# A routed expert layer: rows gathered by a list of nodes instead of scattered to their places

## The chip, the cores and the metric

The kernel runs on one core of a Trainium2 chip. A core has a matrix engine (TensorE, PE), a vector engine (VectorE, DVE), a scalar engine (ScalarE, ACT), a general engine (GpSimd, POOL) and a sequencer that mostly issues transfers (SyncE, SP). Each engine takes its own instructions in order, and engines wait for each other by semaphores. Sixteen DMA engines move data between the large memory (HBM) and the on-chip memory (SBUF). TensorE writes its results to a small accumulation memory (PSUM).

The metric is device microseconds (us) of one execution, as the median over runs. Three runs of the kernel before are given: 5335.9, 5335.99 and 5341.02 us, with a median of 5335.99 us.

## The reference, cut to what matters

The program takes 625 nodes with 512 features and 10,000 edges through eight layers. Each adds its result to the nodes. The change lies in the second of them, an attention block followed by a layer in which each node is sent to one of eight experts:

```python
h = _layernorm(x + o, ln1_g, ln1_b)            # o: output of the attention
t = h.reshape(b * s, d)                        # 625 x 512
probs = jax.nn.softmax(t @ gate_W + gate_b, axis=-1)
idx = jnp.argmax(probs, axis=-1)               # one of 8 experts per node
gw = jnp.max(probs, axis=-1)
hid = jax.nn.gelu(jnp.einsum('nd,edf->enf', t, W1) + b1[:, None, :])
out_all = jnp.einsum('enf,efd->end', hid, W2) + b2[:, None, :]
onehot = jax.nn.one_hot(idx, E, dtype=t.dtype)
out = jnp.einsum('ne,end->nd', onehot, out_all)
out = out * gw[:, None]
```

W1 is 8 x 512 x 2048 and W2 is 8 x 2048 x 512, all in float32.

## The kernel before, in words

The kernel is one program of eight phases, one function each, run one after the other. The nodes stay in SBUF as `C.x`, five tiles of 125 nodes (`NT` = 5, `P` = 125) by 512 features. The second phase is `L0_ffn`.

**Experts with 128 places each.** A node goes only through the expert that its gate chose. Each expert has 128 places (`SLOTS`), so 8 x 128 = 1024 places in all, and a node's place number is `slot` = 128 times its expert plus its rank among that expert's nodes. A node whose rank is 128 or more gets a number of its own beyond 1024 and is left to a second routine, `L0_late`, which runs only if some expert has more than 128 nodes (line 898). `slot` is made on DVE from the one-hot choice `oh` with two small products on PE (lines 784 and 785) that count the nodes before each one; `to` is `slot` as an integer (line 797).

**How the rows reach their experts.** The layer's input rows `t_tok` are in SBUF by node. Lines 798 to 800 scatter them: for each of the five node tiles, one indirect transfer issued by POOL writes 125 rows of 2 KB to `places` in HBM, at the rows that `to` gives. All five write the same HBM tensor. Lines 801 to 803 then load the eight experts' 128 rows from `places` into eight buffers `at_e`, by transfers that SP issues. So that unused places hold numbers, SP fills `places` with zeros early in the phase (lines 724 and 725), beside the zeros for `made`, the HBM tensor that takes the experts' results (lines 726 to 728).

**What follows.** PE turns each expert's rows with four transposes into `xg`, features by places (line 823); DVE and ACT take turns copying the results out of PSUM (lines 179 and 181 in the helper `copy`). Then the experts run. The weights come through a ring of six 1 MB buffers (`ring`, line 682): 64 loads, two for each of 32 steps. The first six are issued at the start of the phase, and each later one is issued when a buffer is released. `first` (line 843) multiplies a step's W1 part, ACT applies the activation (line 848), and `second` (line 857) multiplies the W2 part. The seven first experts' results go to `made`, and `take` (line 872) fetches each node's row from there with five indirect transfers on POOL; the last expert's results are spread by one-hot products (line 881).

**What else the steps below touch.** The attention ends with the layer norm of `t_tok` (`C.layernorm`, lines 153 to 164). The small tensors of the gate live in a pool opened after the attention (`a_r`), whose memory the attention used before, so their first writers wait for the attention. Work is placed on the engines' queues by a scheduler that may move an instruction ahead of or behind others of its engine; the order spoken of in the prediction is the order in the built program. SP's queue holds, in this order, the six ring loads, eight zero fills of `places`, two of `made`, the load of the attention's output weights (`Wo`), the other fills of `made`, the load of the next phase's weights (`w_next`), the eight loads of `at_e`, and the rest of the ring. Two small loads of a much later phase, `wx` and `bsel` (lines 1292 and 1314), are issued by ACT just before the experts start.

Of the kernel before, what the change touches and what calls it, by code (L numbers as in the profile page):

```python
# [15 lines left out]
F32 = mybir.dt.float32  # L16
F16 = mybir.dt.float16
BF16 = mybir.dt.bfloat16
I32 = mybir.dt.int32
U32 = mybir.dt.uint32  # L20
U16 = mybir.dt.uint16
AF = mybir.ActivationFunctionType
ALU = mybir.AluOpType
AX = mybir.AxisListType
# [4 lines left out]
N, D, P, NT = 625, 512, 125, 5  # L29
# [11 lines left out]
SLOTS = 128  # L41
# [614 lines left out]
def L0_ffn(C):  # L656
# [5 lines left out]
    nc, tc, I = C.nc, C.tc, C.ins  # L662
    E8, FF = 8, 2048
# [4 lines left out]
    with ExitStack() as st:  # L668
# [7 lines left out]
        def load(upto):  # L676

            for key in parts[len(loaded):upto]:
# [3 lines left out]
                nc.sync.dma_start(w, src.rearrange("(k p) n -> p k n", p=128))  # L682
                loaded[key] = w


        places = C.dram.tile([E8 * SLOTS + N, D], F32, name="places")
        made = C.dram.tile([E8 * SLOTS + N, D], F32, name="made")
        zero = pool.tile([128, D], F32, name="zero")
        nc.gpsimd.memset(zero, 0.0)
# [2 lines left out]
        t_tok = pool.tile([P, NT, D], F32, name="t_tok")  # L692
        with ExitStack() as st2:
            apool = st2.enter_context(tc.tile_pool(name="aa", bufs=1))
            qT = apool.tile([128, KC, N], F32, name="qT")
            kT = apool.tile([128, KC, N], F32, name="kT")
            v = apool.tile([P, NT, D], F32, name="v")
            with tc.tile_pool(name="a_ps", bufs=2, space=PSUM) as ps:
                xT = apool.tile([128, KC, N], F32, name="xT")
                C.feature_major(ps, xT, xn)  # L700
                bo = C.row_bcast(pool, W("bo"), D, "bias", 2)
                for t in range(NT):
                    nc.gpsimd.tensor_add(xn[:, t], xn[:, t], bo[:P])
                for dst, w, b in ((qT, "Wq", "bq"), (kT, "Wk", "bk")):
                    wt = C.weight(W(w).rearrange("(k p) n -> p k n", p=128), KC)
                    col = C.columns(pool, ps, W(b).rearrange("(c p) -> c p", p=128), KC, "col_" + b)
                    for c in range(KC):
                        for n0, n in HALVES:
                            pq = ps.tile([128, 512], F32, name="pq")
                            C.linear_T(pq[:, :n], xT, n0, n, wt, c)  # L710
                            nc.scalar.activation(dst[:, c, n0:n0 + n], pq[:, :n], AF.Identity,
                                                 bias=col[:, c:c + 1])
                wt = C.weight(W("Wv").rearrange("(k p) n -> p k n", p=128), KC)
                bv = C.row_bcast(pool, W("bv"), D, "bias", 2)
                for t in range(NT):
                    pv = ps.tile([P, D], F32, name="pv")
                    C.linear(pv, xT, t, wt)
                    nc.vector.tensor_add(v[:, t], pv, bv[:P])
            wt = C.weight(W("Wo").rearrange("(k p) n -> p k n", p=128), KC)
            g = C.row_bcast(pool, W("ln1_g"), D, "ln_g")  # L720
            b = C.row_bcast(pool, W("ln1_b"), D, "ln_b")
            st_ = C.small.tile([P, NT, 6], F32, name="ln_st")

            for e in range(E8):
                nc.sync.dma_start(places[e * SLOTS:(e + 1) * SLOTS], zero[:SLOTS])
            for r in range((E8 - 1) * SLOTS, E8 * SLOTS + N, 128):
                n = min(128, E8 * SLOTS + N - r)
                nc.sync.dma_start(made[r:r + n], zero[:n])

            def finish(t, out):  # L730
                for half in range(2):
                    part = xn[:, t, half * 256:(half + 1) * 256]
                    nc.vector.tensor_add(part, part, out[half])
                nc.vector.bn_stats(st_[:, t], xn[:, t])

            C.attention(qT, kT, v, wt, 1.0 / 8.0, False, finish)
            C.layernorm(t_tok, xn, g, b, st_)

        tT = pool.tile([128, KC, N], F32, name="tT")
        sel = pool.tile([P, NT, E8], F32, name="sel")  # L740
# [2 lines left out]
        with ExitStack() as st2:  # L743
            E2 = st2.enter_context
            rpool = E2(tc.tile_pool(name="a_r", bufs=1))
            R = lambda shape, name: rpool.tile(shape, F32, name=name)
            beyond = R([P, NT], "beyond")
            nc.gpsimd.iota(beyond, pattern=[[P, NT]], base=E8 * SLOTS, channel_multiplier=1,
                           allow_small_or_imprecise_dtypes=True)
            place = R([128, E8], "place")  # L750
            nc.gpsimd.iota(place, pattern=[[SLOTS, E8]], base=0, channel_multiplier=1,
                           allow_small_or_imprecise_dtypes=True)
            before = R([P, P], "before")
            nc.vector.tensor_scalar(before, C.iota[:P, :P], place[:P, 0:1], None, op0=ALU.is_gt)
            to = rpool.tile([P, NT], U32, name="to")
            xg = R([128, KC, E8 * SLOTS], "xg")
            srow = R([128, N], "srow")
            slot, rk, gv = R([P, NT], "slot"), R([P, NT], "rk"), R([P, NT], "gv")
            oh, rank, base = (R([P, NT, E8], k) for k in ("oh", "rank", "base"))
            with tc.tile_pool(name="a_ps3", bufs=2, space=PSUM) as ps, tc.tile_pool(name="a_at", bufs=1) as work:  # L760
# [35 lines left out]
                nc.vector.tensor_add(slot, slot, beyond)  # L796
                nc.vector.tensor_copy(to, slot)
                for t in range(NT):
                    nc.gpsimd.indirect_dma_start(out=places[:, :], in_=t_tok[:, t], in_offset=None,
                                                 out_offset=bass.IndirectOffsetOnAxis(ap=to[:, t:t + 1], axis=0))  # L800
                at_e = [work.tile([SLOTS, D], F32, name="at_e", bufs=E8) for e in range(E8)]
                for e in range(E8):
                    nc.sync.dma_start(at_e[e], places[e * SLOTS:(e + 1) * SLOTS])
                top = pool.tile([1, 1], F32, name="top")
                nc.vector.tensor_add(base[0:1, 0], base[0:1, NT - 1], pn[0:1, 1, NT - 1])
                nc.vector.reduce_max(top, base[0:1, 0], axis=AX.X)
# [944 lines left out]


PHASES = [graph_and_L0_gnn, L0_ffn, L1_gnn, L1_ffn, L2_gnn, L2_ffn, L3_gnn, L3_ffn]


# [48 lines left out]
```

## Time and profile before

| what | us |
|---|---|
| median of three runs | 5335.99 |
| the profiled execution | 5344.59 |
| its span, first to last instruction | 5342.8 |
| TensorE busy over the span | 4977.2 (93%) |
| attention's last products, layer norm, gate and ranks: from 427 to 453 | 26 |
| from the first scatter on POOL (453.07) to the first product with W1 (492.50) | 39.4 |
| experts, to the last product with W2 (about 717) | 224 |

The profile is of one execution. A row names line, engine, operation, and result and operands (`places<-t_tok,to`), then how often and how long. Busy time of TensorE counts a product as busy while it is in flight, and the granted clock (`PEclk`, 1.00 is full speed) says how fast TensorE was allowed to run. `PEld` is the loading of the stationary operand, which TensorE does beside its products. A wait is put down to the engine or transfer that ended it last.

### The profile page before, as it was taken

The page shows a single profiled execution, that of the slowest core. Times are in us where ns is not written, and L with a number is a line of the kernel's source. Part 1 is how long each engine was busy: PE and PEld are TensorE (multiplying, and loading weights), DVE is VectorE, ACT ScalarE, POOL GpSimd, SP SyncE. Part 2 cuts the span into 40 slices and gives each one's busy share as a digit, 9 for nine tenths or more (in the row PEclk, how much of TensorE's full clock was granted, in tenths as well). Part 3 has the DMA queues.
Part 4 walks back from the last instruction along what each step waited for, and adds up shares of the span by engine and source line. Part 5 has one row for each costly group of instructions (what it writes and reads, how often), then busy time and mean ns, then how long its engine had stood idle before and what let it go on. Part 6 is the DMA issues. An engine that isn't in the chain of part 4 may idle for free. (4 is left out here: it accounts for less than half of the span.)

```text
span 5342.8 us, 184932 instructions
## 1 busy us (share of the span) xinstructions
PE 4977.2 (93%) x74524; PEld 3136.7 (59%) x74524; DVE 2688.4 (50%) x13552; ACT 1100.5 (21%) x4479; POOL 61.5 (1%) x57
## 2 busy tenths in 40 slices
PE   9996989999999889999999999999999999999988
PEld 6565745555556555555555555555555555555555
DVE  7542042330035156656666556666566666556258
ACT  8342111110124111111111111111111111111125
POOL 0100010000000000000000000000000000000000
PEclk9997988989989999999999999999999999999988
DMA  1213942311125400000000000000000000000200
GB/s 37 90 54 116 315 142 71 99 53 57 42 85 198 145 1 12 6 6 6 6 6 6 6 6 6 6 7 12 6 6 6 6 6 6 6 6 0 69 12 10
DMA packets 168011, 232.19 MB, mean 43 GB/s; under 512 B 64322, under 2 KB 81079, under 8 KB 167096
## 3 DMA queue, kind: packets, MB, share of 16 engines
q1 hardware_dynamic: 155484, 220.05, 12.7%
q10 hardware_dynamic: 10122, 7.55, 0.6%
q0 software_dynamic: 2240, 2.57, 0.2%
q8 instruction: 81, 1.33, 0.1%
q14 instruction: 84, 0.69, 0.0%
HBM read 196.59 MB, written 33.54 MB: 43 GB/s over the span
## 5 line engine op out<-in xcount | busy, mean ns | idle before, releaser
L1502 PE MATMUL pa<-wp,left 128*23 128x384 bf16 x33312 | 1497.2, 327 | 134.0 <-issue 49.5
L1502 PEld LDWEIGHTS pa<-wp,left 128*23 128x23 bf16 x33312 | 802.5, 93 | 651.5 <-DVE left L1639 152.9
L1531 PE MATMUL po<-wo,left 128*1 128x128 f32 x20000 | 656.2, 273 | 0.0
L1531 PEld LDWEIGHTS po<-wo,left 128*1 128x1 f32 x20000 | 479.4, 84 | 128.4 <-issue 0.3
L1543 PE MATMUL spare<-wo,ident 128*128 128x256 f32 x1250 | 437.4, 431 | 25.5 <-issue 25.5
L1617 DVE STREAM_TRANSPOSE col<-pa 128x384 f32<-128x384 f32 x625 | 349.4, 559 | 196.0 <-PE pa L1502 196.0
L1607 DVE COPY col<-gxb 128x16 f32 x625 | 113.9, 182 | 647.7 <-DVEq L1582 647.7
L1574 ACT ACTIVATE act<-ga 128x12 f32<-128x12 f32 x625 | 132.7, 212 | 1181.8 <-DVE ga L1619 1181.8
L1569 ACT COPY xrow<-xsb 1x4 f32<-1x4 f32 x625 | 120.5, 193 | 1213.0 <-ACTq L1567 1213.0
L1543 PEld LDWEIGHTS spare<-wo,ident 128*128 128x128 f32 x1250 | 186.1, 188 | 166.3 <-issue 166.3
L1344 PE MATMUL pg<-xT,w 128*128 128x312 f32 (+1 forms) x1024 | 274.9, 429 | 1.0 <-DVE sel L1321 0.3
L1344 PEld LDWEIGHTS pg<-xT,w 128*128 128x128 f32 x1024 | 193.6, 190 | 81.9 <-DVE gt L1353 4.4
L1494 PE MATMUL lg<-wso,th 128*1 128x8 f32 x5008 | 216.3, 169 | 16.7
L1490 PE MATMUL lg<-wsel,act 128*1 128x8 f32 x5008 | 216.3, 169 | 1.8 <-DVE act L1628 1.5
L1621 DVE STREAM_TRANSPOSE col<-po 128x128 f32<-128x128 f32 x625 | 198.2, 317 | 27.2 <-PE po L1531 0.9
L1494 PEld LDWEIGHTS lg<-wso,th 128*1 128x1 f32 x5008 | 147.7, 81 | 75.8 <-DVE wso L1631 12.8
L1487 PEld LDWEIGHTS lg<-xrow,ones 1*1 1x1 f32 x1252 | 51.3, 76 | 235.8 <-issue 235.8
L502 PE MATMUL wide<-hot_dst,hot_src 125*125 125x512 bf16 x640 | 177.8, 391 | 12.5 <-DVE hot_dst L482 12.5
L1631 DVE TENSOR_TENSOR wso<-wsel,so 128x32 f32<-128x32 f32 x625 | 119.7, 192 | 119.1 <-ACT so L1576 117.3
L232 PE MATMUL po<-w,hT 128*125 128x512 f32 x400 | 175.1, 592 | 0.0
L1490 PEld LDWEIGHTS lg<-wsel,act 128*1 128x1 f32 x5008 | 147.5, 81 | 46.5 <-DVE act L1628 1.9
L1576 ACT ACTIVATE so<-go 128x4 f32<-128x4 f32 x625 | 128.2, 205 | 216.8 <-DVE go L1626 216.8
(418 smaller groups left out, 6099.2 us busy)
## 6 DMA issues: line engine op xcount, KB each, us to landing
ring<-in_L_ffn_W_dram SPq DMA_DIRECT2D x64, 1024.0 KB
gxb<-gx SPq DMA_DIRECT2D x25, 800.0 KB
w<-in_L_ffn_WihT_dram SPq DMA_DIRECT2D x16, 1024.0 KB
raw<-in_L_ffn_WhhT_dram SPq DMA_DIRECT2D x24, 512.0 KB
gx<-gt SPq DMA_DIRECT2D x16, 626.0 KB
iw<-gates SPq DMA_DIRECT2D x32, 312.5 KB
gx<-gt SPq DMA_DIRECT2D x16, 624.0 KB
w<-in_L_ffn_W_dram SPq DMA_DIRECT2D x32, 256.0 KB
```

Of the source, the lines that this page charges most:

```text
L232: self.nc.tensor.matmul(out, xT[:, k, t * P:(t + 1) * P], w[:, k, :], start=start and k == 0, stop=stop and k == k_n - 1)
L502: nc.tensor.matmul(wide[i], hs[:, k], hd[:, :W0], start=first, stop=last)
L1344: nc.tensor.matmul(pg[:, :n], w[:, k, s * 128:(s + 1) * 128], xT[:, k, n0:n0 + n], start=k == 0, stop=k == KC - 1)
L1490: pe.matmul(lg, c2[:, s:s + 1], wsel[:, 1, s], start=False, stop=False)
L1494: m = pe.matmul(lg, th[:, s:s + 1], wso[:, s], start=False, stop=s == KC - 1)
L1502: m = pe.matmul(pa[32 * j:32 * j + 2 * GAP + 1], upper[:, s], wp[e][:, s, i, j].rearrange("p g n -> p (g n)"), start=k == 0, stop=k == 11, ...
L1531: m = pe.matmul(po[32 * j:32 * j + 1].rearrange("p (u r) -> p u r", r=32), left[:, s, 0:1], wo[e][:, s].rearrange("p (u j r) -> p j u r", ...
L1543: pe.matmul(spare[:, :256], C.ident, wo[0][:, 0, :256], start=True, stop=True)
L1574: act.activation(act4[:, 0:3].rearrange("p g s -> p (g s)"), ga, AF.Tanh, scale=0.5).then_inc(sem["ifg"])
L1576: act.activation(so, go, AF.Sigmoid).then_inc(sem["so"])
L1617: dve.transpose(col[:, :12, :32], pa.rearrange("p (b r) -> p b r", r=32)).then_inc(sem["ta"])
L1621: dve.transpose(col[:, 12:, :32], po.rearrange("p (s r) -> p s r", r=32)).then_inc(sem["to"])
```

## The change

The scatter to `places` and the loads from it are taken out, with the zero fills. Instead:

1. The rows `t_tok` are written to HBM in the order of the nodes (`nodes`), by two plain transfers on SP.
2. On POOL and DVE, the node numbers are prepared as two bfloat16 parts (`ids`: a multiple of 256 and the rest), and a row of the numbers 0 to 1023 (`slots`).
3. For each of the five node tiles DVE makes a one-hot matrix `G` of 125 nodes by 1024 places, in bfloat16.
4. PE multiplies it with `ids`, 8 experts times 5 tiles, so that `pw` holds for each place the two parts of the node's number. DVE adds the parts and makes them integers (`who`). An empty place gets node 0.
5. POOL issues eight indirect transfers, one for each expert, that fetch 128 rows of `nodes` by `who` into `at_e`.

The diff is the whole change:

```diff
@@ -682,8 +682,8 @@
-        places = C.dram.tile([E8 * SLOTS + N, D], F32, name="places")
+        nodes = C.dram.tile([N, D], F32, name="nodes")
@@ -720,9 +720,6 @@
             st_ = C.small.tile([P, NT, 6], F32, name="ln_st")
-
-            for e in range(E8):
-                nc.sync.dma_start(places[e * SLOTS:(e + 1) * SLOTS], zero[:SLOTS])
             for r in range((E8 - 1) * SLOTS, E8 * SLOTS + N, 128):
                 n = min(128, E8 * SLOTS + N - r)
                 nc.sync.dma_start(made[r:r + n], zero[:n])
@@ -735,6 +732,8 @@
             C.attention(qT, kT, v, wt, 1.0 / 8.0, False, finish)
             C.layernorm(t_tok, xn, g, b, st_)
+            for p0, p1 in ((0, 112), (112, P)):
+                nc.sync.dma_start(nodes.rearrange("(t p) d -> p t d", p=P)[p0:p1], t_tok[p0:p1])
@@ -753,6 +752,22 @@
             to = rpool.tile([P, NT], U32, name="to")
+
+            node, part = R([P, NT], "node"), R([P, NT], "part")
+            ids = rpool.tile([P, NT, 2], BF16, name="ids")
+            nc.gpsimd.iota(node, pattern=[[P, NT]], base=0, channel_multiplier=1,
+                           allow_small_or_imprecise_dtypes=True)
+            nc.vector.tensor_scalar(part, node, 256.0, 256.0, op0=ALU.is_ge, op1=ALU.mult)
+            nc.vector.tensor_copy(ids[:, :, 0], part)
+            nc.vector.tensor_sub(node, node, part)
+            nc.vector.tensor_scalar(part, node, 256.0, 256.0, op0=ALU.is_ge, op1=ALU.mult)
+            nc.vector.tensor_add(ids[:, :, 0], ids[:, :, 0], part)
+            nc.vector.tensor_sub(ids[:, :, 1], node, part)
+            slots = rpool.tile([P, E8 * SLOTS], F16, name="slots")
+            nc.gpsimd.iota(slots, pattern=[[1, E8 * SLOTS]], base=0, channel_multiplier=0,
+                           allow_small_or_imprecise_dtypes=True)
+            G = rpool.tile([P, NT, E8 * SLOTS], BF16, name="G")
+            who_f, who = R([SLOTS, E8], "who_f"), rpool.tile([SLOTS, E8], U32, name="who")
@@ -796,11 +811,17 @@
                 nc.vector.tensor_copy(to, slot)
                 for t in range(NT):
-                    nc.gpsimd.indirect_dma_start(out=places[:, :], in_=t_tok[:, t], in_offset=None,
-                                                 out_offset=bass.IndirectOffsetOnAxis(ap=to[:, t:t + 1], axis=0))
+                    nc.vector.tensor_scalar(G[:, t], slots, slot[:, t:t + 1], None, op0=ALU.is_equal)
+                pw = ps.tile([SLOTS, E8, 2], F32, name="pw", bufs=1)
+                for e in range(E8):
+                    for t in range(NT):
+                        nc.tensor.matmul(pw[:, e], G[:, t, e * SLOTS:(e + 1) * SLOTS], ids[:, t], start=t == 0, stop=t == NT - 1)
+                nc.vector.reduce_sum(who_f, pw, axis=AX.X)
+                nc.vector.tensor_copy(who, who_f)
                 at_e = [work.tile([SLOTS, D], F32, name="at_e", bufs=E8) for e in range(E8)]
                 for e in range(E8):
-                    nc.sync.dma_start(at_e[e], places[e * SLOTS:(e + 1) * SLOTS])
+                    nc.gpsimd.indirect_dma_start(out=at_e[e], out_offset=None, in_=nodes[:, :],
+                                                 in_offset=bass.IndirectOffsetOnAxis(ap=who[:, e:e + 1], axis=0))
```

## The prediction

> **What bounds the kernel now.** I read the page first, then busy time by stretches, the list of waits, and the order of time around the change.
>
> ```profile
> span 5342.8 us, 184932 instructions
> ...
> PE   9996989999999889999999999999999999999988
> ```
>
> One engine, TensorE (PE), is busy 93% of the span, so a gain has to come from a place where PE stands idle. The page's 40 slices are too coarse for that (133.6 us each); the stretches of the changed phase show it.
>
> ```profile
> core 0: us, PE busy (x) PEld busy (x) DVE busy (x) ACT busy (x) POOL busy (x), PEclk, DMA share, GB/s
> 427.00:453.00 26.00, 14.95 (x68) 13.89 (x68) 14.30 (x65) 2.88 (x5) 0.00 (x0) 0.57 0.00 1
> 453.00:484.00 31.00, 3.75 (x13) 2.84 (x14) 2.82 (x11) 0.00 (x0) 6.15 (x5) 0.50 0.21 62
> 484.00:492.00 8.00, 7.34 (x32) 5.85 (x30) 2.82 (x5) 1.89 (x4) 0.00 (x0) 0.50 0.53 184
> 492.00:532.00 40.00, 39.49 (x240) 29.93 (x241) 1.03 (x3) 8.57 (x26) 0.00 (x0) 1.00 0.83 279
> ```
>
> From 453 to 484 PE works 3.75 of 31 us, and no other engine is busy either: all wait for transfers. From 492 on, the experts keep PE busy without a gap and at full clock (1.00). So whatever moves the first product with W1 (line 843) moves everything after it. The waits name the cause:
>
> ```profile
> engine line waited for: us in total, times, longest us
> ...
> PE pt L823 <- DMA at_e<-places: 26.5, 2, 26.0
> ...
> POOL places L799 <- DMA places<-t_tok,to: 17.5, 4, 4.6
> ```
>
> PE waits 26 us for an expert's rows, and before that each scatter on POOL waits for the one before it, because all five write one tensor. In order of time:
>
> ```profile
> 452.57 0.17 DVE L797 CAST to<-slot 125x5 uint32<-125x5 f32 x1
> ...
> 453.07 1.39 POOL L799 DMA_INDIRECT places<-t_tok,to  x1 [26.10 <-DVE junk L815]
> ...
> 475.54 1.19 POOL L799 DMA_INDIRECT places<-t_tok,to  x1 [4.25 <-DMA places<-t_tok,to]
> 480.89 3.64 SPq L803 DMA_DIRECT2D at_e<-places  x8
> 483.63 1.57 PEld L823 LDWEIGHTS pt<-ident,at_e 128*128 128x128 f32 x8 [26.39 <-issue]
> ...
> 492.50 7.22 PEld L843 LDWEIGHTS ph<-xg,ring 128*128 128x128 f32 x64 [1.08 <-ACT xg L179]
> ```
>
> Places known 452.74, first row block at PE 483.63, first W1 product 492.50. The nearest row for the new gathers is `take`, whose five indirect fetches go to different columns:
>
> ```profile
> 699.22 1.24 POOL L872 DMA_INDIRECT yt<-made,to  x1 [222.49 <-SPq L898]
> 700.76 1.22 POOL L872 DMA_INDIRECT yt<-made,to  x1 [0.30 <-issue]
> ...
> 705.32 1.55 POOL L872 DMA_INDIRECT yt<-made,to  x1 [0.30 <-issue]
> ```
>
> They start every 1.53 us, not every 5.6, and the first reader on DVE starts 5.7 to 5.8 us after the issue (699.22 to 705.0).
>
> **What the Trainium skill says.** "TensorE: Matmul & The Clock Gate", Part 1: TensorE runs at half clock until an activity window of about 3.4 us was busy, and falls back after an idle one. The trace agrees: 0.50 from 449 to 492, 1.00 from 492.05, after the transposes had run without a gap since 486.09. The clock's steps at 17.6, 430.7 and 492.05 lie on one grid of 3.41 us. "DMA: Bandwidth & Descriptors", Anatomy of one DMA: the fixed part of a POOL transfer is about 2 us and mostly the receipt, worst with HBM as target. Here a scatter to HBM lands 5.3 us after its issue, 1.2 of them POOL's own; no fetch into SBUF beside idle DMA engines is shown.
>
> **The change, part by part.**
>
> *Removed.* Five scatters in a row, the loads from `places` and 2 MB of zero fills. The fills lie at 260 to 272, where PE is 40 of 40 us busy on products from SBUF: no gain. In SP's new order `Wo` stands behind `w_next`, but it waits for a buffer that PE frees at 276.9 (issued 276.96 before); ring and fills then end about 9 us earlier. No loss.
>
> *Writes of `nodes`.* Two on SP, behind `Wo`, waiting for the last `t_tok` (about 435). A like pair (`graph_sym`, 1.56 MB) kept the DMA engines busy for 6 us, so 1.28 MB lands near 441; the gathers ask for it 20 us later. Behind them on SP stands only the ring, whose buffers are not free before the experts start. Free.
>
> *Preparing `ids` and `slots`.* POOL: two more index rows; a 625-wide one takes 0.65 us, and POOL has nothing else. DVE: six tiny operations, and line 754 moved, now between the last attention sum and the end of the layer norm, where DVE sets the pace (427.7 to 434.7). Most fit in the 0.2 us between dependent small operations; line 754 (0.29 us, beginning under the sum's tail) and three behind line 163 do not. **+0.6 us** (0.2 to 1.1).
>
> *One-hots.* Same form as line 482 (float16 in, bfloat16 out, a column as scalar): 388 ns at 625 wide, line 475 252 ns at 125 wide, so 0.272 ns a column. The skill's "VectorE: DVE Perf Modes", perf-mode tier table, gives such an operation four elements a cycle (0.26 ns), which agrees. 1024 wide: 0.50 us, and line 482's follower starts 0.29 us after it, so 0.39 for 1024. Four times 0.39 plus 0.50 = **2.1 us**, from 453.25 (452.65, where line 815 starts now, plus 0.6) to 455.3.
>
> *Forty products.* Expert by expert, so the first needs all five tiles; four run ahead. Each is a 128-column load and a product two columns wide. PE is at half clock, and a load sets the pace: the skill ("TensorE: Matmul & The Clock Gate", LDWEIGHTS) gives columns / 1.2 ns = 107 ns. In the trace cold bfloat16 loads follow each other by 0.11 us, and the gate's float32 products (line 232, 8 wide, cold) by 0.215, two such. 36 x 0.107 = 3.9, plus 0.25 for the last to finish: **459.4**. Bounds 0.06 (warm) and 0.215 a pair: 2.2 to 7.7 us; I take the row's half.
>
> *`who`.* The sum takes 0.2 us. In DVE's order a copy of `srow` stands before the last step, and waits 0.83 us for its own product behind the forty: 460.3, plus 0.17, plus 0.33 from DVE to POOL as `to` has now: first gather at **460.8**. Lines 815 to 834, also later, end under the gathers.
>
> *Gathers.* In the built order only the first one carries a wait. Eight of 1.53 us: the last is issued at 460.8 + 10.7 = 471.5. Reader after the issue: 5.7 us in `take` under 300 GB/s of ring traffic; with idle DMA engines 4.2 (1.2 to issue, 2.7 from SP's loads' issue to PE, 0.3) is the low end. I take 5.2: **476.7**. Then four transposes and a copy, 1.63 us as now (490.87 to 492.50): line 843 at **478.3**, 14.2 us earlier.
>
> *Clock.* The transposes come every 1.53 us and take 0.95, so PE is 62% busy, and the grid's window from 485.2 to 488.6, with PE 2.9 of 3.4 us busy, did not raise the clock. So I expect line 843 to start at half clock and to need one whole window: 3.4 to 6.8 us, 5.1 on average. Its products go at 0.116 us warm, transposes of that shape at 0.24 cold; lost 5.1 x (1 - 0.116 / 0.24) = **2.6 us** (0 to 3.4).
>
> *Later.* The `wx` and `bsel` loads now stand at the phase's end behind the last products, and their two DVE operations in the next layer norm: **+0.3 us**. They land about 726 at 3.4 us after issue; DVE asks at 727.6. Late by x, they cost x.
>
> Sum: -14.2 + 2.6 + 0.3 = **-11.3 us** (the 0.6 is inside). The profiled execution (5344.6) would be 5333.3. Nothing in the sum depends on what makes it 8.6 us longer than the median, so 5335.99 - 11.3 = **5324.7 us**.
>
> **Rivals.**
>
> *The gain is there, but under 0.2% (10.7 us, about what a measurement of this kernel can tell from no change).* Forty pairs at 0.215 (+3.9), 5.7 us per gather (+0.5), a clock low for 6.8 us (+0.8) and `wx` late by 0.5 leave 5.6 us: 5330.4. For it: each bound has a row. Against it: they need not come together. Half of them suffice, so it is near.
>
> *The gathers run one by one, slower.* If POOL started each only when the one before has landed, as the scatters do (5.6 us apart), the last is issued at 500.0 and line 843 starts near 506.8: +14.3, +2.9 as above, 5353. It decides from a spacing of (492.5 - 2.9 - 1.63 - 5.2 - 460.8) / 7 = 3.1 us. Against it: eight different buffers, a source that is only read, no wait in the order, and `take` at 1.53. For it: eight in a row are more than `take` shows.
>
> *The experts' stage is bound by the weights' transfers.* It moves 67 MB with a DMA share of 0.83 to 0.92. If starting earlier only met the weights earlier, nothing would be won: 5336. But six buffers are full since before 300, the next load starts on a release, and PE has no gap; the stream moves with it.
>
> *PE warm and quick transfers*: 5320, the forecast's good end.
>
> **How the numbers follow.** Forecast with its good end, 0.58; gain under 0.2%, 0.31; weights bind, 0.04; one by one or another loss, 0.07. Faster by over 0.2% 0.58, within 0.35, slower 0.07. Range: good end, -2.6 for the clock, -1.0 for the gather, -1.7 for warm pairs: 5319.4; bad end 5330.4; runs differ by up to 5 us, so I add 1 below and 2 above: 5318 to 5333.
>
> **What would show it.** Right: line 823's first wait ends near 466, POOL's gathers 1.5 us apart from about 461, line 843 at about 478, PEclk 0.50 there for some us. Wrong: gathers over 3 us apart; the forty products above 5 us; gaps in PE among the experts; DVE waiting for `wx` in the next layer norm.

## The result and the profile after

The kernel after took 5313.07 us (5310.64 to 5320.02, six executions) against 5335.94 for the kernel before on the same chip: a ratio of 0.9958, 95% interval 0.9946 to 0.9971. That is 22.9 us won, 15 to 29 by the interval, where 11.3 were forecast. Later comparisons of the same two kernels gave 20.5 us (0.9959, 0.9944 to 0.9974) and 19.6 us (0.9963, 0.9949 to 0.9976).

The head of the page after, and the busy time by stretches (columns as before: length, busy time of each engine with its instructions, granted TensorE clock, share of the transfer engines, GB/s):

```profile
span 5308.5 us, 185014 instructions
```

```profile
core 0: us, PE busy (x) PEld busy (x) DVE busy (x) ACT busy (x) POOL busy (x), PEclk, DMA share, GB/s
427.00:453.00 26.00, 14.02 (x65) 13.34 (x65) 14.77 (x72) 2.88 (x5) 1.26 (x4) 0.54 0.16 50
453.00:460.00 7.00, 4.96 (x50) 3.74 (x50) 3.95 (x16) 0.00 (x0) 2.73 (x3) 0.50 0.16 42
460.00:470.50 10.50, 8.10 (x32) 5.75 (x32) 3.41 (x6) 2.02 (x4) 5.06 (x6) 0.53 0.54 172
470.50:510.50 40.00, 39.63 (x241) 30.08 (x242) 0.69 (x1) 8.44 (x26) 0.00 (x0) 1.00 0.85 278
```

Of the 31 us in which every engine waited, 7 are left, with work in them; then 10.5 us in which the rows arrive and are transposed, and then the experts. The list of waits has no entry of 26 us for an expert's rows any more:

```profile
engine line waited for: us in total, times, longest us
...
PE pt L844 <- DMA at_e<-nodes,who: 2.2, 5, 0.8
POOL at_e L823 <- issue: 2.1, 7, 0.3
```

In order of time (start, length, engine, line, operation, in brackets the idle time before it):

```profile
452.01 0.17 DVE L812 CAST to<-slot 125x5 uint32<-125x5 f32 x1
452.09 2.06 DVE L814 TENSOR_SCALAR G<-slots,slot 125x1024 bf16<-125x1024 f16 x5
...
454.21 1.03 PEld L818 LDWEIGHTS <-G 125*128 125x128 bf16 x36 [0.29 <-DVE G L814]
...
456.66 1.17 POOL L823 DMA_INDIRECT at_e<-nodes,who  x1 [28.37 <-DVE who L820]
458.13 0.96 POOL L823 DMA_INDIRECT at_e<-nodes,who  x1 [0.30 <-issue]
...
465.63 0.95 POOL L823 DMA_INDIRECT at_e<-nodes,who  x1 [0.30 <-issue]
...
470.87 7.41 PE L864 MATMUL ph<-xg,ring 128*128 128x128 f32 x64 [0.67 <-ACT xg L179]
```

From the cast of the places (line 812; 797 before) the first product with W1 (864; 843 before) is 18.9 us away instead of 39.9. From here on I count from that cast, since the cast itself lies anywhere from 450.2 to 455.0 us, for reasons that come before it:

| us from the cast | forecast | before, two profiles | after, three profiles |
|---|---|---|---|
| first gather | 7.6 | - | 4.65, 4.65, 4.65 |
| last gather | 18.3 | - | 13.6, 13.6, 13.6 |
| first product with W1 | 25.1 | 39.9, 38.3 | 18.9, 19.2, 19.2 |
| its first 64 products take | 10.0 | 7.4, 7.4 | 7.4, 9.9, 10.3 |
| last sum of the stage | 257.6 | 269.8, 268.2 | 248.7, 251.5, 252.0 |

(The forecast's 257.6 is 25.1, the 229.9 us that the kernel before needs from its first product to the last sum, and 2.6 for the clock.) The stage is 18.3 us shorter on the mean, 269.0 less 250.7.

### The profile page after: what moved, and what is told of

The parts are those of the page before. It is cut to its first block, busy times and chain, and to the rows that moved or that the text cites. A ratio compares the mean times of both kernels' runs of the same rounds, so it can differ in the third digit from the quotient of the medians.

```text
span 5308.5 us, 185014 instructions
## 1 busy us (share of the span) xinstructions
PE 4970.8 (94%) x74564; PEld 3130.1 (59%) x74564; DVE 2692.5 (51%) x13565; ACT 1100.2 (21%) x4479; POOL 64.1 (1%) x62
## 5 line engine op out<-in xcount | busy, mean ns | idle before, releaser
L1523 PE MATMUL pa<-wp,left 128*23 128x384 bf16 x33312 | 1498.0, 328 | 127.4 <-issue 39.1
L1564 PE MATMUL spare<-wo,ident 128*128 128x256 f32 x1250 | 437.6, 432 | 25.7 <-issue 25.7
```

Source lines behind the costliest of these rows:

```text
L1523: m = pe.matmul(pa[32 * j:32 * j + 2 * GAP + 1], upper[:, s], wp[e][:, s, i, j].rearrange("p g n -> p (g n)"), start=k == 0, stop=k == 11, ...
L1564: pe.matmul(spare[:, :256], C.ident, wo[0][:, 0, :256], start=True, stop=True)
```

## The experiments

All are the kernel after with one edit, but for the moved transposes, which are built up in steps. Times are compared with the kernel before in the same group of executions. Four of them (125 columns, 125 rows, 112 rows, weights beside the gathers) were run once, for their profile: their times are too few to compare.

**Gathers that wait for one another**

```diff
-                nc.vector.tensor_copy(who, who_f)
+                nc.vector.tensor_copy(who[:, 0:1], who_f[:, 0:1])
...
+                nc.vector.scalar_tensor_tensor(who[:, e:e + 1], at_e[e - 1][:, 0:1], 0.0, who_f[:, e:e + 1],
+                                               op0=ALU.mult, op1=ALU.add)
```

> The list of nodes is made as in the kernel after, but each gather now waits until the one before it has landed, because the number column of expert e+1 is written by VectorE from the landed rows of expert e. Theory (the gain is that transfers which waited for one another now overlap): spacing is landing 3.75 us plus about 0.4 us on VectorE and GpSimd, 4.2 us instead of 1.25; the last gather starts at about 486 us, line of the first expert products at about 491.7 us instead of 470.9, and the time comes back to 5334 us (5329 to 5340), the whole gain gone. Rival (the gain comes from the zero fills taken out, the fewer bytes in memory or the earlier phases, and the overlap only adds a little): the time stays below 5322 us.

```profile
462.89 0.95 POOL L827 DMA_INDIRECT at_e<-nodes,who  x1 [3.08 <-DVE who L825]
466.48 0.16 DVE L825 SCALAR_TENSOR_TENSOR who<-at_e,who_f 128x1 uint32<-128x1 f32 x1 [2.30 <-DMA at_e<-nodes,who]
...
466.91 0.94 POOL L827 DMA_INDIRECT at_e<-nodes,who  x1 [3.06 <-DVE who L825]
...
491.74 9.68 PE L871 MATMUL ph<-xg,ring 128*128 128x128 f32 x64 [0.68 <-ACT xg L179]
```

The gathers start 4.0 us apart, the first product stands at 491.74 (491.7 expected), and the stage lasts 269.8 us, as long as before (269.8 and 268.2). The first product comes 37.7 us after the cast, against 39.9 and 38.3 before, and its low clock then takes 2.3 back (9.68 us for the first 64 products instead of 7.41). The median is 5334.38 against 5339.06, 0.9992 (0.9983 to 1.0001). So within the stage the gain is the overlap, to within about 2 us: gathering by a list saves next to nothing when each gather waits for the one before it. That the median is still 4.7 us lower is taken up below.

**125 one-hot columns instead of 128**

```diff
-                        nc.tensor.matmul(pw[:, e], G[:, t, e * SLOTS:(e + 1) * SLOTS], ids[:, t], start=t == 0, stop=t == NT - 1)
-                nc.vector.reduce_sum(who_f, pw, axis=AX.X)
+                        nc.tensor.matmul(pw[:P, e], G[:, t, e * SLOTS:e * SLOTS + P], ids[:, t], start=t == 0, stop=t == NT - 1)
+                nc.vector.reduce_sum(who_f[:P], pw[:P], axis=AX.X)
```

> The forty products that make the list load 125 one-hot columns an expert instead of 128 (the last three slots of each expert are left out and read as node 0). Theory (the weight load is quick because it is exactly 128 columns wide of a 2-byte type, and the forecast took its price from loads of 125 columns): 0.10 to 0.11 us from load to load, so the last 36 products take 3.6 to 3.9 us instead of 1.12 and the first gather starts 2.5 to 2.8 us later, counted from the cast of the places. Rival (a product two columns wide is quick by itself, and the forecast's row was slow for another reason, such as its 512-wide products): 36 products in 1.1 to 1.3 us as before, first gather 4.6 to 4.8 us after the cast.

```profile
454.63 3.91 PEld L819 LDWEIGHTS <-G 125*125 125x125 bf16 x36 [0.21 <-DVE G L815]
...
459.96 1.17 POOL L824 DMA_INDIRECT at_e<-nodes,who  x1 [31.11 <-DVE who L821]
```

36 loads take 3.91 us instead of 1.03: 0.109 against 0.029 each, at half clock both. The first gather comes 7.52 us after the cast (452.44) instead of 4.65. Three columns fewer cost 2.9 us. The Trainium skill says so ("TensorE: Matmul & The Clock Gate", Weight-path perf modes): loads of exactly 128 weights of a type other than FP32 are fast, four times in theory for 8-bit weights and about twice as measured there. Here, with bfloat16, it is 3.8 times.

**125 and 112 rows a gather, and weights loaded beside the gathers** (the edit for 125; for 112 the two `:P` are `:112`)

```diff
-                    nc.gpsimd.indirect_dma_start(out=at_e[e], out_offset=None, in_=nodes[:, :],
-                                                 in_offset=bass.IndirectOffsetOnAxis(ap=who[:, e:e + 1], axis=0))
+                    nc.scalar.activation(at_e[e][96:], zero[96:], AF.Identity)
+                    nc.gpsimd.indirect_dma_start(out=at_e[e][:P], out_offset=None, in_=nodes[:, :],
+                                                 in_offset=bass.IndirectOffsetOnAxis(ap=who[:P, e:e + 1], axis=0))
```

> Each gather fetches 125 rows instead of 128 (rows 96 to 127 of the buffer are filled with zeros by ScalarE first; the last three slots of an expert are left out). The forecast took the spacing of 1.53 us from the gathers at the end of the stage, which fetch 125 rows while expert weights are being loaded. Theory (the other transfers make those slow): GpSimd stays at 0.95 us a gather, spacing 1.25, landing 3.5 to 4.0 us. Rival (a count of rows that is no multiple of 16 or 128 makes it slow): GpSimd 1.2 us, spacing 1.5, landing above 4.5 us.

```profile
L824 POOL DMA_INDIRECT at_e<-nodes,who x8: 1211/1211/1389, 458.1 to 468.8; - x8
...
DMA to landing us min/median/max: 5.5/5.8/6.1
```

My theory fell. With little else on the transfer engines, 125 rows take 1.21 us of GpSimd and land in 5.8 us, much like the gathers at the end of the stage (1.22 and 5.4 before). So I asked which numbers of rows are quick:

> Each gather fetches 112 rows (the last 16 slots of each expert are left out and read as zero). A gather of 128 rows took GpSimd 0.95 us and landed in 3.5 to 4.0, one of 125 took 1.21 and landed in 5.5 to 6.1, with little else on the transfer engines. Theory (rows are dealt evenly over 16 engines only when their number is a multiple of 16): 112 rows take 0.8 to 0.95 us and land in 3.3 to 4.0. Rival (only the full 128 rows are quick): 1.1 us or more and 5 us or more.

```profile
L824 POOL DMA_INDIRECT at_e<-nodes,who x8: 929/933/1141, 460.2 to 469.1; - x8
...
DMA to landing us min/median/max: 3.3/3.3/3.3
```

112 go like 128. The view of the transfers shows the difference, packets by size in the stretch of the eight gathers, for 125 rows, 112 rows, and 128 rows (the repeat of the kernel after):

```profile
DMA packets 1792, 2.06 MB, mean 111 GB/s; under 512 B 1272, under 2 KB 1272, under 8 KB 1792
```

```profile
DMA packets 640, 1.84 MB, mean 136 GB/s; under 512 B 128, under 2 KB 128, under 8 KB 640
```

```profile
DMA packets 640, 2.10 MB, mean 150 GB/s; under 512 B 128, under 2 KB 128, under 8 KB 640
```

A gather of 128 or of 112 rows is 80 packets, 16 of them small; one of 125 is 224, 159 of them small. The five scatters before, 125 rows each, are 224 packets apiece too (1120 for five) and land in 5.3 us. The Trainium skill ("DMA: Bandwidth & Descriptors", Why a DMA increments its semaphore by 16 and not by 1) says that a transfer is dealt to the largest number of engines up to 16 that divides the size of its slowest dimension, here the rows, with an exception for some direct copies. That fits the order found (128 and 112 divide by 16, 125 does not). How many engines the 125 rows used, and what the small packets are for, no run here shows.

```diff
+                for n in ("Wq", "Wk", "Wv", "Wo"):
+                    C.weight(W(n).rearrange("(k p) n -> p k n", p=128), KC, behind=who_f[0:1, 0:1])
```

> Four loads of 1 MB, whose data nobody uses, start when the list is ready and so run beside the gathers. Theory (traffic sets the price of the gathers at the end of the stage): while the loads run, GpSimd takes about 1.2 us a gather, spacing 1.5, and landing 5 us or more, so that the first expert products start 3 to 5 us later after the cast of the places than in the kernel after (18.9 us there). Rival (traffic does not matter to either): 0.95 us, 1.25 us and 3.5 to 4.0 us stay. Third outcome: landing longer with GpSimd unchanged, which says that the two figures have different causes.

The third outcome: GpSimd stays at 0.95 us and the spacing at 1.25, but the rows land in 7.7 to 9.8 us, and the first product comes 25.0 us after the cast. In these runs the number of rows changes the spacing, and rows and traffic both change the landing.

**The clock: the kernel after again, the kernel before again, and TensorE's gaps filled**

> The kernel after, unchanged, with a new profile. Of five profiles of this form (after, serial, 125 columns, 125 rows, loaded) only that of after had the TensorE clock at full before the first 64 expert products (7.41 us); in the others it rose 2.9 to 5.6 us into them (9.0 to 10.3 us). Theory (TensorE is busy 86% of the time ahead of them, which is at the limit, so that the clock rises early in some executions only): either 7.4 or 9 to 10.3 us here, with all else the same: 4.6 us from cast to first gather, spacing 1.25, landing 3.5 to 4.0, 18.9 us from the cast to the first expert products. Rival (the after kernel's shorter gaps raise the clock each time): 7.4 us again. Time 5313 to 5319 us.

> The kernel before, unchanged, with a new profile. In the first one the clock rose 0.5 us ahead of the first 64 expert products, which took 7.41 us. Theory (TensorE is 86% busy ahead of them, at the limit, in both kernels): 7.4 or 9 to 10.3 us here, and from the cast of the places to the stage's last sum 270 to 273 us. Rival (the kernel before has the clock up each time and the kernel after mostly has not, so that the change costs 2.5 us of clock as forecast): 7.4 us again and 269.8 us. Time 5332 to 5341 us, a ratio of 1.

> The kernel after once more, as the reference of this call. Theory (the clock is raised ahead of the expert products in a minority of its executions): 9 to 10.3 us for the first 64 products, as in four of the five profiles that kept its order of transposes with no weights beside them. Ratio to before 0.9955 to 0.9962.

The first 64 products in the repeats of the kernel after (first and second fence) and of the kernel before (third):

```profile
470.97 9.92 PE L864 MATMUL ph<-xg,ring 128*128 128x128 f32 x64 [0.68 <-ACT xg L179]
```

```profile
473.32 10.34 PE L864 MATMUL ph<-xg,ring 128*128 128x128 f32 x64 [0.68 <-ACT xg L179]
```

```profile
488.52 7.41 PE L843 MATMUL ph<-xg,ring 128*128 128x128 f32 x64 [0.68 <-ACT xg L179]
```

The first profile after was the exception. Counting all kernels here that leave this stretch as it is or change it by rows or columns only, the clock was up ahead of the products in one of eight profiles (9.9 to 10.3 us in the others), and in both of the kernel before, whose last 24 transposes come in one burst of 4.5 to 5.7 us. So the rival of the second expectation holds in both profiles. Theory for the cause: the gaps between landings. Filling them:

```diff
                 for e in range(E8):
+                    nc.tensor.matmul(spare[:, :64], at_e[e][:, :128], C.ones[:, :64], start=True, stop=True)
...
+                for _ in range(3):
+                    nc.tensor.matmul(spare[:, :128], at_e[E8 - 1][:, :128], C.ones, start=True, stop=True)
```

> The kernel after with eleven products more that nobody reads: one of 64 columns ahead of each expert's transposes and three of 128 columns behind the last, to fill TensorE's gaps between landing and landing. Theory (the clock rises after a stretch without gaps): it rises ahead of the first expert products, whose first 64 take 7.4 us instead of 9 to 10; they start at most 1 us later (19 to 20 us after the cast of the places), so 1.5 us less at the end of the stage. Rival (gaps of 0.2 to 0.7 us are not what keeps the clock low): 9 us or more again, and the stage ends as late or up to 1 us later.

TensorE and its clock in the 10.4 us ahead of the first products, for the repeat of the kernel after and with the gaps filled:

```profile
460.60:471.00 10.40, 8.31 (x33) 0.50 0.50 156
```

```profile
461.50:471.90 10.40, 9.43 (x55) 0.73 0.52 154
```

With 9.43 us busy instead of 8.31 the clock rose on the way, the 64 products took 7.38, and the stage 249.0 us instead of 251.5 to 252.0. That agrees with the Trainium skill ("TensorE: Matmul & The Clock Gate", Part 1), by which a free-running window of about 3.4 us has to be busy, and which calls the result variable from run to run. It is one profile, and how busy TensorE is does not settle it alone: in the 3.41 us before the clock rose in the first profile after (466.37 to 469.78) it was busy for 2.98 us, while in the second repeat it was busy for 3.05 of 3.41 us (469.26 to 472.67) and the clock stayed low. So the cause is made likely by the filling, but not shown. The time went the other way, 5326.59 us against 5343.2 (0.9970, 0.9958 to 0.9982). In its one profile the recurrence, more than 1100 us later, took 3100.7 us from its first to its last row, against 3085.2 to 3090.5 in the three profiles of the kernel after. Why was not followed up, so this is no better version.

**Zero fills kept**

```diff
+        places = C.dram.tile([E8 * SLOTS + N, D], F32, name="places")
...
+            for e in range(E8):
+                nc.sync.dma_start(places[e * SLOTS:(e + 1) * SLOTS], zero[:SLOTS])
```

> The kernel after with the eight zero fills of a buffer of 3.4 MB kept, which nothing reads. Theory (the fills are off every path, as the forecast took them): the times and the stretch up to the cast of the places as in the kernel after, 5313 to 5319 us. Rival (a part of the gain is the fills' 2 MB of writes and their room on the queue): 3 us or more slower, and a cast of the places later than 455 us.

5320.52 us against 5343.2 in that group: 0.9959 (0.9944 to 0.9975), the same ratio as in the first repeat of the kernel after. The cast came at 453.9, inside the spread of the others. No gain from leaving out the fills is seen. (The 5320 is 1.5 us above what was expected; the kernel before was 6 us slower in that group than in the one before, so the ratio decides.)

**Transposes between the products**

In the kernel after, the first products wait for the eighth gather and all transposes. They could start on the first expert's rows.

```diff
+            def turned(e):
+                pt = acc[e % NT]
+                for k in range(KC):
+                    nc.tensor.transpose(pt[:, k * SLOTS:(k + 1) * SLOTS], at_e[e][:, k * 128:(k + 1) * 128], C.ident[:SLOTS, :SLOTS])
+                C.copy(e, xg[:, :, e * SLOTS:(e + 1) * SLOTS], pt[:, :KC * SLOTS].rearrange("p (k n) -> p k n", k=KC))
...
             for i, (e, q) in enumerate(steps):
                 first(e, q)
+                if q == 1 and e < E8 - 1:
+                    turned(e + 1)
```

`turned(0)` stands ahead of the loop, the old transposes are gone, the bank of an output sum that is not yet in use takes the transposes, `at_e` is kept in eight tiles of its own for the whole stage, and `G` moves to memory that is given back ahead of the experts.

> The transposes of an expert's rows move from ahead of all expert products to between them: those of expert 0 alone stand ahead of the first product, those of expert e+1 after the second quarter of expert e. Theory (in the kernel after the first products wait for the last gather, so 7 of the 8 gathers can be hidden): first expert products at about 10.5 us after the cast of the places instead of 18.9, at half clock, of which the first 64 take 9 to 11 us instead of 7.4; the stage ends 5 to 8 us earlier than in the kernel after, time about 5307 us (5302 to 5312). Rival (the moved transposes and copies stand in the products' way, and weights that load beside the gathers make them land late): the expert products from first to last take 5 us or more longer, and the time is 5312 us or more.

> As with the moved transposes, and the node numbers are made before attention instead of behind the layer norm. Theory: 0.4 to 0.7 us less between the last products of attention and the cast of the places (26.6 us in the kernel after, 25.9 before), else the same; time 0.5 us below that of the moved transposes alone, which is within what can be measured. Rival (the order table of slots on GpSimd, which stays, is what slowed VectorE there): 26.3 us or more.

The stage did as expected: 245.3 us in both, and the second, which also prepares `ids` ahead of the attention, shows 26.13 us from the last attention copy to the cast instead of 26.55. But the medians were 5319.07 and 5315.44, beside 5316.5 for the kernel after. Behind the stage, in the profile with the moved transposes:

```profile
704.47 0.35 ACTq L1317 DMA_DIRECT2D wx<-in_L_ffn_WselT_dram  x1
...
713.67 0.18 DVE L1319 TENSOR_SCALAR wx<-wx 128x32 f32<-128x32 f32 x1 [9.18 <-DMA wx<-in_L_ffn_WselT_dram]
...
715.31 2.37 DVE L160 TENSOR_SCALAR xn<-x,ln_mv,ln_r 125x512 f32<-125x512 f32 x5 [0.41 <-DVE ln_r L123]
```

A load of 16 KB for a layer far ahead, moved behind the branch and behind 1.5 MB of the graph, holds VectorE for 9.2 us in the middle of a layer norm. The theory: the new tiles had moved the memory that `wx` will lie in, and with it the place of its load. So the rows went into buffers that nobody reads by then, and `G` back to where the kernel after has it:

```diff
+        at_e = [xn_[:, e] if e < NT else t_tok_[:, e - NT] for e in range(8)]
```

(`xn_` and `t_tok_` are the two buffers, widened to 128 rows.)

> As with the moved transposes, but the gathered rows lie in the buffers of the attention's residual and of the normed tokens, which are no longer read by then, and not in new memory. In the runs with moved transposes the stage ended 6 us earlier (245.3 us from the cast of the places to its last sum, 251.5 in the repeat of the kernel after), and the next layer norm then waited 9.2 us on VectorE for the 16 KB of wx, whose load had moved behind the branch on ScalarE and behind 1.5 MB of the graph. Theory (the new memory shifted where wx lies, and with it the place of its load): the load of wx stands ahead of the branch again, VectorE does not wait for it, 114 to 117 us from the stage's last sum to the first products of the next feed-forward instead of 121 to 124, and the time is 5308 to 5313 us, 5 to 7 us less than the kernel after in the same state of the clock. Rival (the earlier end of the stage itself makes the load late): the wait stays, 120 us or more, and 5315 us or more.

```profile
701.05 0.15 DVE L1321 TENSOR_SCALAR wx<-wx 128x32 f32<-128x32 f32 x1
...
706.23 2.37 DVE L160 TENSOR_SCALAR xn<-x,ln_mv,ln_r 125x512 f32<-125x512 f32 x5 [0.53 <-DVE ln_r L123]
```

No wait for `wx`; the next rows are normed 10.5 us after the stage's last sum instead of 16.3. (Two tiles changed their place here, so which of them had moved the load is not told apart.) The stage took 244.8 us, the time is 5309.63 against 5343.2: 0.9937 (0.9923 to 0.9950). The stretch to the next feed-forward, though, was 119.2 us and not 114 to 117: TensorE's clock stayed low there until 795 us, as it did in the repeat of the kernel after (120.0).

**The moved loads of `wx` and `bsel`**

Already in the kernel after these two loads stand behind the last products. Here the one-hots and `slots` lie in memory that is given back ahead of the experts, which puts the loads where the kernel before has them, alone and together with the moved transposes.

```diff
-            G = rpool.tile([P, NT, E8 * SLOTS], BF16, name="G")
+                G = work.tile([P, NT, E8 * SLOTS], BF16, name="G")
```

(`slots` likewise.)

> The kernel after with the one-hots and the row of slots in memory that is given back ahead of the experts; with that the loads of wx and bsel stand on ScalarE where the kernel before has them, and not behind the last products. The forecast gave the moved loads 0.3 us. From the stage's last sum (its last start) to the normed rows of the next layer the profiles show 8.4 and 7.7 us before, 9.9, 11.4 and 10.0 after. Theory (the two loads hold up ScalarE's branch, and with it the square root of the layer norm): 7.6 to 8.5 us here, about 2.4 less than the kernel after, with the stage itself as long as there (248.7 to 252.0 us from the cast of the places). Rival (ScalarE's lateness there comes from the earlier time or from the traffic, not from the moved loads): 9.9 us or more.

> The moved transposes with the rows gathered into the two buffers that are no longer read, and the loads of wx and bsel in their old place. Theory: a stage of 244 to 246 us from the cast of the places, 7.6 to 8.5 us from its last sum to the next normed rows, and a time 8 to 10 us below the kernel after in the same call. Rival (the transposes between the products cost the next phases what they win, as in the first try): a time within 3 us of the kernel after.

From the last sum to the normed rows: 8.4 and 7.7 us before; 9.9, 11.3 and 9.8 after; 9.9 with the loads early; 8.3 with the moved transposes too. The first theory is not borne out by the run made for it: its time of 5312.50 us is 5.0 below the kernel after, with intervals that overlap widely (0.9938 to 0.9965 against 0.9949 to 0.9976), but not by way of this stretch. The second run alone fits the theory. The loss is there (10.3 less 8.0 on the mean, 2.3 us); that the two loads cause it stays open. The second run took 5305.62 us, against 5337.09 before (0.9944, 0.9931 to 0.9958) and 5317.47 for the kernel after in the same group, 11.9 us less. The two intervals against before still overlap a little, and by its ratio the version is not told apart from the one with moved transposes above (0.9937), so which is the best stays open.

**What lies outside the stage**

> The gathers that wait for one another once more, with more rounds. In the first run its stage was as long as before (269.9 us against 269.8 and 268.2), it has the later loads of wx (2.4 us) and the longer layer norm (0.65), and yet its median was 4.7 us below that of the kernel before (interval of the ratio 0.9983 to 1.0001). Theory (that was chance): a ratio of 0.9998 to 1.0012. Rival (some 5 us are won outside the stage by every kernel with the change, as the sum over the stage, 15 us, against the measured 20 to 23 suggests): a ratio of 0.9985 to 0.9995, with an upper end below 1.

5332.77 against 5337.09, 0.9992 (0.9983 to 1.0000). By the mark set ahead the ratio is the rival's, and the upper end just touches 1. Twice now a kernel whose stage is as long as before came out more than 4 us below it, although it also has the longer preparation and the longer stretch to the next normed rows (9.9 us). The profiles point to the recurrence, where nothing was changed: 3091.5 and 3095.2 us before, 3084.9 and 3085.9 in these two, 3087.1, 3085.2 and 3090.5 after.

One wait in it tells the kernel before from all the others. VectorE there waits for a group of products of TensorE (line 1502; 1523 after), here before and after (us in total, times):

```profile
  DVE col L1617: 196.0, 139
```

```profile
  DVE col L1638: 189.4, 140
```

The repeats give 197.4 before and 188.9 and 190.7 after, the two serial kernels 188.2 and 187.2, and all sixteen profiles with the change lie between 186.6 and 192.2. So about 7 us less are waited in the kernel after, and about 9 in the serial one. It is not the whole story: the kernels with the fills (192.2) and with the filled gaps (189.6) wait less as well and still have the longest recurrences (3096.2 and 3100.7 us), and the stretches ahead of the recurrence and behind it differ by 5 to 8 us between profiles of the same kernel. What in the changed phase reaches this place was not tested; the cause is open.

## Why the prediction was wrong

The direction and the mechanism held: one transfer waiting for another was the cost, and overlap is the gain. What failed is the size of two terms, the forty products and the gathers, and a term put at nothing: the forecast let nothing change behind the stage but the loads of `wx` and `bsel`.

- *Preparing `ids` and `slots`, +0.6:* 25.9 and 25.7 us from the last attention copy to the cast before, 26.6 after: +0.8. Right. *One-hots, 2.1 us:* 2.06. Right. *Fills and the writes of `nodes` free:* no cost or gain of theirs is seen. Right.
- *Forty products, 36 x 0.107 us:* wrong. They took 0.03 each. The row taken was of 125-column loads (line 502, 125x125 bfloat16), and even the lower bound (0.06) did not reach it. This is 2.9 us of the 3.0 by which the first gather came earlier than forecast.
- *Gathers of 1.53 us:* wrong by the row. `take` moves 125 rows, the new gathers 128: 1.25 us, so 1.7 to 2.0 over seven of them. *Reader 5.2 us after issue:* 3.5 to 4.0 to landing, so some 1.3. The forecast laid `take`'s latency to ring traffic of 300 GB/s. That was a misreading of the kernel before: while its `take` runs (699 to 712 us), all other transfers (q1) move half as much as the gathers themselves (q0; packets, MB, share), and the mean of both is 152 GB/s:

```profile
q0 software_dynamic: 1120, 1.29, 34.3%
q1 hardware_dynamic: 344, 0.67, 13.7%
```

- *First product 14.8 us earlier, counted from the cast:* 20.0 (39.1 less 19.1).
- *Clock, 2.6 lost:* right, though the first profile after shows none. The three of that kernel lost 0, 2.5 and 2.9.
- *`wx` and `bsel`, +0.3:* 2.3 lost there, with the cause not settled. They did not come late for VectorE, as the forecast feared; the square root on ScalarE came late.
- *Nothing else behind the stage:* wrong, and the largest of the three; see the next sum.

Sum: 18.3 us in the stage, less 0.8, less 2.3, makes 15.2, where the forecast's 14.8 - 2.6 - 0.6 - 0.3 made 11.3. Inside what it looked at, the forecast thus missed some 3.9 us. The two wrong rows gave 6.0, of which 0.8 go because the second profile of the kernel before reached its first product earlier than the one that the forecast starts from. A clock that lost 1.8 on the mean gave 0.8, and `wx` and the preparation took 2.2 back.

With these 15.2 us the forecast would have been 5320.8, still inside its range. The measured 19.6 to 22.9 hold another 4.4 to 7.7, and they carried the result below 5318. By the same sum the serial kernel holds some 8, for its stage, its preparation and its stretch to the next normed rows (9.9 us) add about 3.4 us and it came out 4.3 to 4.7 lower. The shorter wait of VectorE in the recurrence, 7 and 9 us, is of this size. That it makes up the rest is an estimate from these profiles and not shown.

Of the rivals, the gain under 0.2% fell with the two wrong rows, and the weights did not bind where the stage begins: TensorE was busy 39.63 of its first 40 us. Gathers one by one were priced at 5353 us; the kernel in which each waits for the one before gave 5334 and 5333, since their spacing was 4.0 us and not 5.6.

## What to carry to other kernels

Before a transfer is priced by another one's row, compare the number of rows as well as the bytes: 125 rows of 2 KB cost 1.21 us of GpSimd and 5.8 to land, 128 cost 0.95 and 3.6. The same goes for a load of bfloat16 weights, where 125 columns took nearly four times as long as 128. And when a change moves tiles in memory, read the order of loads on every queue behind the stage too: a 16 KB load for a later layer held VectorE for 9.2 us, and the 6 us won in the stage did not show in the time. What lies outside the stage can weigh as much as a term of the forecast: compare the waits of the unchanged phases too.

## What the runs showed of the hardware

- An indirect transfer of 112 or 128 rows, both multiples of 16, is quicker than one of 125: 80 packets instead of 224, landing in 3.3 and 3.6 us instead of 5.8. Other numbers of rows were not run.
- One-hot products of 128 bfloat16 columns by 2 run at 0.03 us a pair at half clock, those of 125 columns at 0.11.
- Four 1 MB loads beside the gathers lengthen their landing from 3.6 to 9.6 us and leave GpSimd's time as it is.
